# A two-layer network on one core: the first layer's normalisation in its own stretch of slot 6, other slots for its pieces, and the first fronts among the recurrence's last lead steps

## The chip, the core and the metric

The kernel runs on one core of a Trainium2 chip. The core has five engines, each with an instruction queue of its own that is worked off in order: TensorE (PE, matrix products; its weight loads are listed apart as PEld), VectorE (DVE), ScalarE (ACT, tabulated functions), GpSimd (POOL) and SyncE (SP), which here only issues DMA transfers. The engines meet at semaphores. The metric is the device time of one execution in microseconds; the time before is the median of three runs.

## The reference

The input is x, 4 images of 128 channels on 64 by 64 points. Two layers are computed, each with a spatial and a token part, all with residual connections:

```
x = x + conv0(ln_c(x))                 # deformable neighbourhood attention
t = t + recurrence(ln_t(t))            # y_t = sigmoid(wx_t + y_{t-1} V^T), 4096 tokens in turn
x = x + mamba(ln_c(x))                 # 8 state-space layers in turn
t = t + experts(ln_t(t))               # 64 experts, 8 tokens of the sequence each
```

Three parts matter here. The recurrence is a chain of 4096 steps for 4 images, each a 128 by 128 product and a sigmoid (in the kernel a tanh). The mamba part takes the recurrence's result, normalises it over the channels (mean, variance, division by the root of the variance plus 1e-6), and sends it through 8 layers. Each layer projects to 2 times 256 channels, convolves 4 taps along the tokens, applies silu, projects to dt, B and C, and runs for each of 256 channels and 16 states the scan h = exp(dt A) h + dt x B along all 4096 tokens; the output is the sum of h C over the states plus D x, gated with silu(z), projected back to 128 channels and put through an RMS norm. After the eighth layer the result is added to the mamba part's input. All is float32.

## The kernel before

**Stages.** `conv_layer` runs first (to about 1.65 ms), then `mamba`, which carries the recurrence with it, then `experts`. In `conv_layer` and `mamba` the order of each engine's instructions is the order in which they are written (`tc.manual_schedule`), so queues can be followed in the code. Waits between engines, and those for a buffer to come free, are put in by the framework. A buffer of a tag with one copy is given to a new tile once all uses of the tile before are done, uses written further down among them.

**Bodies.** Tokens are cut into 8 chunks of 512 (`TL`). A body is one chunk of one layer of one image; 8 x 8 x 4 = 256 bodies run in the order chunk, layer, image. The main loop runs over bodies i, and each iteration has 16 slots j. `o` is the body whose scans run (i), `n` the next, whose front is computed meanwhile, `q` the last, which is finished, and `s` and `z` are the bodies two and three on, if they are in the first layer: those must be fetched and normalised from the recurrence's result, while other layers take the RMS norm's result `us[b]`. `m` is the body two on in any layer, `a` is any body that exists.

In each slot the loop writes: `decay(o, j+2)` (two exponentials on ScalarE), `inputs(o, j+1)` (16 small matmuls into PSUM, the tile dBx; in slots 6 and 7 instead exponentials into the same buffers, dAp, since GpSimd makes the inputs of that pair of states), a recurrence step where `STEPS[j]` is over 0, `scan(o, j)` (two scans on VectorE), after odd j `times_c` (a copy of the last states, then a 128x2048 product on GpSimd that waits for the two scans), the left side of PLAN's row j, `add_up` (eight transposing matmuls that add states to yT), the right side of the row, and a second step where `STEPS[j]` is 2.

**PLAN** is the hand-written table of the remaining pieces, one row per slot, as `who.piece`. The pieces that matter here: `v0`, `v1` project the convolution's input, and ScalarE takes it from the bank with the last tap, then three one-column operations (L851) that add what the previous chunk's last tokens give (`edge`, eight small GpSimd operations, L829 to L836), then a copy of the tail (L855); the `tap` pieces on VectorE (L860) follow. `pz`, `silu`, `silu_z` make the gate; `pd`, `keep` project to dt, B, C; `pt`, `softplus` make dt (L928); `dtx` is the product dt x on GpSimd (L934), `turn` its transposition (L941, then ScalarE L944), `diag` makes diagonal matrices of B for dBx. `po` is the output projection (L1086), `square` reads it twice on ScalarE (L1092, L1094), `pm`, `log`, `rstd`, `u` are the RMS norm (L1098 to L1109), `end` adds the mamba input after the last layer (a load on SP, a GpSimd sum L1115, a store). `s.mean` is the mean's matmul, the subtraction (L812) and the square; `s.var` the variance's matmul (L818) and its logarithm (L819), `s.rstd` the exponential of it, `s.u` the product (GpSimd, L1109). `ln` and `exp` load ScalarE's tables (L1126) for logarithm with exponential, and for exponential with tanh.

**Banks.** Two PSUM banks, f0 and f1, serve all pieces; `BANK` says which takes which. `square` must have read f0 (po) before `pz0` may write it.

**Recurrence.** `rec.step(t)` is a matmul of two instructions (L669) and a tanh (L672), each waiting for the other. Every 64 steps one matmul (L664) puts the inputs into PSUM, and after the last of them GpSimd forms y and the sum (L678, L679) and SP stores it to `x2_d`. Body 0 needs the first 512 tokens; `PRE` = 576 steps run before any of the mamba part. Then bodies 0 and 1 are fetched and normalised, and the `n` pieces of PLAN are run through once for body 0, before the main loop.

Of the kernel before, what the change touches and what calls it, by code (L numbers as in the profile page):

```python
# [9 lines left out]
AF = mybir.ActivationFunctionType  # L10
# [10 lines left out]
B = 4  # L21
# [24 lines left out]
TL = 512  # L46
# [8 lines left out]
PRE = 512 + RT  # L55
# [555 lines left out]
class Recurrence:  # L611
# [78 lines left out]


PLAN = """
n.v0 |
s.mean |
| n.tap03 n.tap02 o.C3
n.v1 | q.leave1 o.by0
n.tap01 | o.by1 q.back1
q.gate1 |
| n.tap12 q.po0 n.tap13 n.tap11
q.po1 | q.square n.pz0 n.pz1 n.silu n.silu_z0 n.silu_z1 a.exp  # L700
n.pd0 | n.pd1 n.keep
n.pt0 n.C2 n.pt1 | n.softplus0 q.pm n.softplus1 a.ln q.log q.rstd s.var s.rstd a.exp
n.dtx0 n.bt n.B |
q.u s.u | o.leave0 n.diag0
q.end n.turn0 n.skip0 n.skip1 | n.diag2
o.back0 n.diag5 | n.diag3
n.diag1 z.fetch n.C0 o.gate0 n.dtx1 m.edge | n.C1
n.diag4 n.turn1 n.diag6 |
""".strip().split("\n")
STEPS = [1, 0, 1, 2, 1, 1, 1, 0, 1, 0, 1, 0, 2, 2, 2, 1]  # L710

BANK = {
    "v0": 0, "v1": 1, "pz0": 0, "pz1": 1, "pd": 0, "pt0": 1, "pt1": 0, "bt": 0, "turn0": 1,
    "turn1": 1, "back0": 1, "back1": 0, "po": 0, "pm": 1, "mean": 1, "var": 1,
}


# [9 lines left out]
def mamba(tc, ops, I, rec, x2_d, x3_d):  # L727
# [8 lines left out]
    nc = tc.nc  # L736
# [5 lines left out]
    with ExitStack() as ctx:  # L742
# [41 lines left out]
        def bank(what):  # L784

            name = f"f{BANK[what]}"
            return psf.tile([P, TL], F32, tag=name, name=name)

        def where(j):

            h, sp = divmod(j, SP)
            return (sp if h == 0 else SP - 1 - sp), h
# [5 lines left out]
        def load(l):  # L798
            given = wp.tile([P, W_GIVEN], F32, tag="given", name="given")
            nc.sync.dma_start(out=given, in_=I["m_given"][l])  # L800
            weights[l] = given


        def fetch(o):
            o.x2 = w1.tile([P, TL], F32, tag="x2", name="x2")
            nc.sync.dma_start(out=o.x2, in_=x2_d[:, o.b, o.ck * TL : (o.ck + 1) * TL])
# [8 lines left out]
        def var(o):  # L815
            o.r = w1.tile([P, TL], F32, tag="r0", name="r0")
            v = bank("var")
            nc.tensor.matmul(v, ops.avg, o.x2, start=True, stop=True)  # L818
            nc.scalar.activation(o.r, v, AF.Ln, bias=ops.eps6)  # L819


        def edge(o):

            o.edge = w.tile([P, NH, DC - 1], F32, tag="edge", name="edge")
            part = w.tile([P, NH, DC - 1, DC - 1], F32, tag="part", name="part")
            for h in range(NH):
                tl = tail[:, o.l, o.b, h, :]
                for k in range(DC - 1):
                    nc.gpsimd.tensor_tensor(  # L829
                        part[:, h, k, :],  # L830
                        tl[:, k : k + DC - 1],
                        taps[:, o.l, h, k : k + 1].to_broadcast([P, DC - 1]),
                        ALU.mult,
                    )
            nc.gpsimd.tensor_tensor(o.edge, part[:, :, 0, :], part[:, :, 1, :], ALU.add)
            nc.gpsimd.tensor_tensor(o.edge, o.edge, part[:, :, 2, :], ALU.add)  # L836
# [132 lines left out]
        def exps(o, j):  # L969
            sp, h = where(j)  # L970
            for k in range(2):
                n = 2 * sp + k
                nc.scalar.activation(  # L973
                    o.dA[j][:, k, :], o.dt[h], AF.Exp, scale=A[:, o.l, h, n : n + 1]
                )

        def decay(o, j):
            if where(j)[0] != SP_B:
                o.dA[j] = dap.tile([P, 2, TL], F32, tag="dA", name="dA")
                exps(o, j)  # L980
# [141 lines left out]
        def get(i):  # L1122
            return bodies[i] if 0 <= i < len(bodies) else None

        def table(name):
# [12 lines left out]
        pieces |= {f"by{h}": lambda o, h=h: times_b(o, SP - 1 + h) for h in range(NH)}  # L1138
        pieces |= {f"C{g}": lambda o, g=g: give_c(o, g) for g in range(NS // 4)}
        pieces |= {  # L1140
            "fetch": fetch, "mean": mean, "var": var, "silu": silu_x, "keep": keep, "B": give_b,
            "bt": turn_b, "square": square, "pm": rms, "log": log, "rstd": rstd, "u": norm,
            "end": lambda o: end(o) if o.l == DEPTH - 1 else None, "edge": edge,
            "exp": table(EXP_TANH), "ln": table(EXP_LN),
# [7 lines left out]
                    pieces[what](who[k])  # L1152

        load(0)
        for t in range(PRE):
            rec.step(t)
        for s in bodies[0:2]:
            for what in ("fetch", "mean", "var", "rstd", "u"):
                pieces[what](s)
        fetch(bodies[2])  # L1160
        edge(bodies[0])
        for row in plan:
            for part in row:
                for k, what in part:
                    if k == "n":
                        pieces[what](bodies[0])
        decay(bodies[0], 0)
        decay(bodies[0], 1)
        edge(bodies[1])
        inputs(bodies[0], 0)  # L1170
        LAG = 4
        t = PRE
        for i in range(len(bodies) + 1):
            o, n, q, s = get(i), get(i + 1), get(i - 1), get(i + 2)
            who = {"o": o, "n": n, "q": q, "m": s, "a": o or q}
            z = get(i + 3)
# [172 lines left out]
@with_exitstack  # L1349
def tile_kernel(ctx: ExitStack, tc: tile.TileContext, I, out):  # L1350
    nc = tc.nc
    const = ctx.enter_context(tc.tile_pool(name="const", bufs=1))
    dram = ctx.enter_context(tc.tile_pool(name="scratch", bufs=1, space=DRAM))
    nc.scalar.preload_act_table_set(EXP_LN)
    ops = Ops(nc, const)
    stats = const.tile([P, B * NBLK, 6], F32, name="stats")
    x1_d = dram.tile([P, B, L], F32, name="x1_d")
    x2_d = dram.tile([P, B, L], F32, name="x2_d")
    x3_d = dram.tile([P, B, L], F32, name="x3_d")
    wx_d = dram.tile([P, B, L], F32, name="wx_d")  # L1360

    with tc.manual_schedule(), ExitStack() as c:
        conv_layer(tc, ops, I, x1_d, wx_d, stats)
        rec = Recurrence(c, tc, ops, I, stats, wx_d, x1_d, x2_d)
        mamba(tc, ops, I, rec, x2_d, x3_d)
    experts(tc, ops, I, x3_d, out)
# [88 lines left out]
```

## Time and profile before

| | |
|---|---|
| median of 3 runs | 16217.22 us (16211.93 to 16219.21) |
| profiled execution | 16205.68 us, span 16203.7 us |
| PE busy | 14711.5 us (91%) |
| DVE busy | 13670.0 us (84%) |
| POOL busy | 13219.3 us (82%) |
| ACT busy | 12120.7 us (75%) |
| scans, L1028 (8192) | 9931 us, 1.26 us each |
| times_c, L1044 (2048) | 9298.0 us, 4.54 us each |
| table loads, L1126 (771) | 989.2 us, 1.283 us each |
| waits of L818 for the logarithm L1102 | 108.3 us over 58 waits (PE and PEld) |
| waits of L941 for dtx | 244.3 us (PE) |
| waits of scans for dBx | 1012.0 us |

A busy time is the sum over an engine's instructions; it is an average over stages, so a share of 84% in the whole can be no gap at all in one stage. The lists of instructions in order of time, one engine at a time, show for each group its start, its duration, its line, what it writes and reads, how many were merged, and in brackets how long the engine stood idle before it and which engine's instruction ended that. "issue" is idle time that no recorded event explains.

### The profile page before, as it was taken

The page shows a single profiled execution, that of the slowest core. Times are in us where ns is not written, and L with a number is a line of the kernel's source. Part 1 is how long each engine was busy: PE and PEld are TensorE (multiplying, and loading weights), DVE is VectorE, ACT ScalarE, POOL GpSimd, SP SyncE. Part 2 cuts the span into 40 slices and gives each one's busy share as a digit, 9 for nine tenths or more (in the row PEclk, how much of TensorE's full clock was granted, in tenths as well). Part 3 has the DMA queues.
Part 4 walks back from the last instruction along what each step waited for, and adds up shares of the span by engine and source line. Part 5 has one row for each costly group of instructions (what it writes and reads, how often), then busy time and mean ns, then how long its engine had stood idle before and what let it go on. Part 6 is the DMA issues. An engine that isn't in the chain of part 4 may idle for free. (4 is left out here: it accounts for less than half of the span.)

```text
span 16203.7 us, 303591 instructions
## 1 busy us (share of the span) xinstructions
PE 14711.5 (91%) x120710; PEld 11053.2 (68%) x120710; DVE 13670.0 (84%) x14929; ACT 12120.7 (75%) x23622; POOL 13219.3 (82%) x9102
## 2 busy tenths in 40 slices
PE   7889689999999999999999999999999999899967
PEld 3444567777777777777777777777777777666636
DVE  8988059998999899989998999889998999899931
ACT  6887258887888788878887888778877887777750
POOL 4554059998999899989999999999998999899940
PEclk8999579999999999999999999999999999999975
DMA  0000012222222222222222222222222222222214
GB/s 21 24 22 20 14 67 101 100 100 99 101 101 101 97 101 101 101 99 98 101 101 103 98 98 100 107 97 99 100 101 102 99 101 97 103 97 99 95 47 121
DMA packets 461738, 1431.35 MB, mean 88 GB/s; under 512 B 205472, under 2 KB 238880, under 8 KB 329120
## 3 DMA queue, kind: packets, MB, share of 16 engines
q1 hardware_dynamic: 460320, 1411.92, 24.4%
q8 instruction: 953, 15.61, 0.4%
q14 instruction: 465, 3.81, 0.1%
HBM read 1353.04 MB, written 58.72 MB: 87 GB/s over the span
## 5 line engine op out<-in xcount | busy, mean ns | idle before, releaser
L1028 DVE TENSOR_TENSOR_SCAN hs<-dA,state,dBx 128x512 f32<-128x512 f32 x7168 | 8702.5, 1263 | 1048.8 <-PE dBx L995 1012.0
L1044 POOL TENSOR_TENSOR hs<-hs,Cb 128x2048 f32<-128x2048 f32 x2048 | 9298.0, 4540 | 166.2 <-POOL state L1041 1.3
L973 ACT ACTIVATE dA<-dt,A 128x512 f32<-128x512 f32 x7168 | 4737.3, 722 | 7.3 <-DVE hs L1028 1.1
L1048 PE MATMUL yT<-ident,hs 128*128 128x128 f32 x32768 | 4349.1, 277 | 7.5 <-POOL hs L1044 7.5
L1048 PEld LDWEIGHTS yT<-ident,hs 128*128 128x128 f32 x32768 | 3794.6, 144 | 770.5 <-issue 643.4
L995 PE MATMUL dBx<-diag,dtxT 64*128 64x128 f32 x57344 | 4188.7, 285 | 122.2 <-DVE hs L1028 109.8
L995 PEld LDWEIGHTS dBx<-diag,dtxT 64*128 64x128 f32 x57344 | 3514.8, 188 | 1085.7 <-issue 711.3
L672 ACT ACTIVATE z<-p 128x4 f32<-128x4 f32 x4096 | 711.6, 174 | 1844.5 <-PE p L669 1838.8
L669 PE MATMUL p<-z,vt 128*128 128x4 f32 x8192 | 1578.9, 263 | 205.6 <-ACT z L672 203.7
L669 PEld LDWEIGHTS p<-z,vt 128*128 128x128 f32 x8192 | 1350.6, 207 | 588.0 <-ACT z L672 304.3
L1016 POOL TENSOR_TENSOR hs<-Bb,dtx 128x512 f32<-128x512 f32 x1024 | 1275.3, 1279 | 0.2 <-PE yT L1048 0.2
L1028 DVE TENSOR_TENSOR_SCAN hs<-dAp,state,hs 128x512 f32<-128x512 f32 x1024 | 1228.5, 1262 | 0.0
L961 DVE TENSOR_TENSOR diag<-f,i 128x512 f32<-128x512 f32 x1792 | 1158.5, 671 | 8.0 <-PE f L949 8.0
L860 DVE SCALAR_TENSOR_TENSOR xc<-f,taps,xc 128x509 f32<-128x509 f32 (+2 forms) x1536 | 1131.0, 736 | 37.6 <-ACT tail L855 10.4
L1041 POOL COPY state<-hs 128x4 f32<-128x4 f32 x2048 | 389.5, 190 | 832.0 <-DVE hs L1028 831.1
L1126 ACT ACT_TABLE_LOAD x771 | 989.2, 1283 | 10.4
L278 DVE SCALAR_TENSOR_TENSOR acc<-qp,dww,acc 128x512 f32<-128x512 f32 x1184 | 888.0, 750 | 12.2
L973 ACT ACTIVATE dAp<-dt,A 128x512 f32<-128x512 f32 x1024 | 708.8, 692 | 212.2 <-DVE hs L1028 180.1
L875 PE MATMUL f<-u,given 128*128 128x512 f32 x1024 | 510.8, 621 | 330.2 <-ACT pos L1094 323.2
L849 ACT ACTIVATE xc<-f,taps 128x509 f32<-128x509 f32 x512 | 350.4, 684 | 474.4 <-PE f L846 472.2
L934 POOL TENSOR_TENSOR dtx<-dt,xc 128x512 f32<-128x512 f32 x512 | 651.8, 1273 | 12.1 <-ACT dt L928 12.1
L944 ACT COPY dtxT<-f 128x512 f32<-128x512 f32 x512 | 298.3, 583 | 448.4 <-PE f L941 448.4
(222 smaller groups left out, 16824.6 us busy)
## 6 DMA issues: line engine op xcount, KB each, us to landing
Cb<-c_d SPq DMA_DIRECT2D x1024, 1024.0 KB, 4.7
Bb<-c_d SPq DMA_DIRECT2D x256, 512.0 KB, 5.5
given<-in_m_given_dram SPq DMA_DIRECT2D x64, 640.0 KB, 5.9
x<-x_d SPq DMA_DIRECT2D x128, 256.0 KB, 2.8
w<-in_w_dram SPq DMA_DIRECT2D x128, 256.0 KB, 2.8
x_d<-x SPq DMA_DIRECT2D x64, 256.0 KB, 2.0
c_d<-dbl SPq DMA_DIRECT2D x512, 32.0 KB, 1.6
xb<-in_x_dram SPq DMA_DIRECT2D x32, 256.0 KB, 3.1
```

Of the source, the lines that this page charges most:

```text
L278: nc.vector.scalar_tensor_tensor(rows(to), x, dww[:, t : t + 1], rows(o.acc), ALU.mult, ALU.add)
L669: nc.tensor.matmul(self.p[:, k, :], self.vt, self.before, start=False, stop=True, skip_group_check=True)
L672: nc.scalar.activation(self.z[:, k, :], self.p[:, k, :], AF.Tanh, scale=0.5)
L860: nc.vector.scalar_tensor_tensor(x, o.v[h][:, : TL - k], taps[:, o.l, h, DC - 1 - k : DC - k], x, ALU.mult, ALU.add)
L961: nc.vector.tensor_tensor(o.diag[:, sp], bt.unsqueeze(2).to_broadcast([P, NB, 64, 2]), i64.unsqueeze(1).unsqueeze(3).to_broadcast([P, NB, ...
L973: nc.scalar.activation(o.dA[j][:, k, :], o.dt[h], AF.Exp, scale=A[:, o.l, h, n : n + 1])
L995: nc.tensor.matmul(o.dBx[j][:, at : at + 64, :], o.dtxT[h][row, n, :], o.diag[row, sp, n], start=True, stop=True,)
L1016: nc.gpsimd.tensor_tensor(hs[:, k, :].rearrange("p (q n t) -> p q n t", n=NB, q=2), o.Bb[:, k, :].rearrange("p (q n t) -> p q n t", n=NB, ...
L1028: nc.vector.tensor_tensor_scan(hs[:, k, :], o.dA[j][:, k, :], hs[:, k, :] if sp == SP_B else o.dBx[j][:, :, k], state[:, o.l, o.b, h, s : ...
L1044: nc.gpsimd.tensor_tensor(hs, hs, o.Cb[f], ALU.mult)
L1048: nc.tensor.matmul(o.yT[:, n, :], x[:, n * P : (n + 1) * P], ops.ident, start=start and n == 0, stop=True, is_transpose=True, skip_group_c ...
L1126: return lambda o: nc.scalar.preload_act_table_set(name)
```

## The change

In PLAN several pieces change their slots. `edge` is computed for the next body in slot 0 rather than for the body two on in slot 14. The variance's matmul moves from slot 9 to slot 6 and from bank f1 to f0; its logarithm is a piece of its own, `lnv`, and stands with its exponential between two table loads (`s.ln`, `s.exp`) in slot 6. `s.u` moves from slot 11 to slot 14, behind `dtx1`; `end` from slot 12 to slot 14, ahead of `dtx1`; the fetch of the first layer's next body from slot 14 to slot 8. Before the main loop only 512 steps of the recurrence run alone. The other 64 are written two at a time after the normalisation of bodies 0 and 1 and after each part of PLAN's rows for body 0; the table loads of the rows (`a` pieces) are run there too, and one after each of the two normalisations.

```diff
 PLAN = """
-n.v0 |
+n.edge n.v0 |
 s.mean |
 | n.tap03 n.tap02 o.C3
 n.v1 | q.leave1 o.by0
 n.tap01 | o.by1 q.back1
 q.gate1 |
-| n.tap12 q.po0 n.tap13 n.tap11
+s.var | n.tap12 q.po0 n.tap13 s.ln s.lnv s.rstd s.exp n.tap11
 q.po1 | q.square n.pz0 n.pz1 n.silu n.silu_z0 n.silu_z1 a.exp
-n.pd0 | n.pd1 n.keep
-n.pt0 n.C2 n.pt1 | n.softplus0 q.pm n.softplus1 a.ln q.log q.rstd s.var s.rstd a.exp
+n.pd0 | z.fetch n.pd1 n.keep
+n.pt0 n.C2 n.pt1 | n.softplus0 q.pm n.softplus1 a.ln q.log q.rstd a.exp
 n.dtx0 n.bt n.B |
-q.u s.u | o.leave0 n.diag0
-q.end n.turn0 n.skip0 n.skip1 | n.diag2
+q.u | o.leave0 n.diag0
+n.turn0 n.skip0 n.skip1 | n.diag2
 o.back0 n.diag5 | n.diag3
-n.diag1 z.fetch n.C0 o.gate0 n.dtx1 m.edge | n.C1
+n.diag1 q.end n.C0 o.gate0 n.dtx1 s.u | n.C1
 n.diag4 n.turn1 n.diag6 |
...
-    "turn1": 1, "back0": 1, "back1": 0, "po": 0, "pm": 1, "mean": 1, "var": 1,
+    "turn1": 1, "back0": 1, "back1": 0, "po": 0, "pm": 1, "mean": 1, "var": 0,
...
             nc.tensor.matmul(v, ops.avg, o.x2, start=True, stop=True)
-            nc.scalar.activation(o.r, v, AF.Ln, bias=ops.eps6)
+            o.var = v
+
+        def log_var(o):
+            nc.scalar.activation(o.r, o.var, AF.Ln, bias=ops.eps6)
...
         load(0)
-        for t in range(PRE):
-            rec.step(t)
+        t = 0
+        def steps(n):
+            nonlocal t
+            for t in range(t, min(t + n, PRE)):
+                rec.step(t)
+                t += 1
+        steps(TL)
         for s in bodies[0:2]:
-            for what in ("fetch", "mean", "var", "rstd", "u"):
+            for what in ("fetch", "mean", "var", "lnv", "rstd", "u", "exp"):
                 pieces[what](s)
+            steps(2)
         fetch(bodies[2])
         edge(bodies[0])
         for row in plan:
             for part in row:
                 for k, what in part:
-                    if k == "n":
+                    if k in ("n", "a"):
                         pieces[what](bodies[0])
+                steps(2)
+        steps(PRE)
```

More of the change, by code (lines that the diff above doesn't have):

```diff
@@ L1140, in mamba @@
         pieces |= {
-            "fetch": fetch, "mean": mean, "var": var, "silu": silu_x, "keep": keep, "B": give_b,
+            "fetch": fetch, "mean": mean, "var": var, "lnv": log_var, "silu": silu_x, "keep": keep, "B": give_b,
             "bt": turn_b, "square": square, "pm": rms, "log": log, "rstd": rstd, "u": norm,
@@ L1171, in mamba @@
         LAG = 4
-        t = PRE
         for i in range(len(bodies) + 1):
```

## The prediction

> **What bounds the kernel now.** I read the page, then the waits, then the timeline engine by engine. The chain that ended last covers only the closing experts stage and says nothing of the edits. The 256 bodies fill 2203 to 15640 us. I measured their lengths by the ACT copy of L895, one per body: an ordinary body takes 50.8 us (every fourth 51.5; mean 50.97), and the five around each turn from the last layer to the first take 54.7, 58.3, 59.0, 60.2 and 55.6 (means of the turns). A turn so costs 33 us more than five ordinary bodies, and there are seven. Slots are PLAN's rows, from 0.
>
> VectorE, first an ordinary body, then twice one with first-layer pieces (start us, us, engine, line, tiles; in brackets the idle time before it and who ended it):
>
> ```profile
> 8057.47 2.45 DVE L1028 TENSOR_TENSOR_SCAN hs<-dA,state,dBx 128x512 f32<-128x512 f32 x2 [2.58 <-PE dBx L995]
> 8777.00 2.45 DVE L1028 TENSOR_TENSOR_SCAN hs<-dA,state,dBx 128x512 f32<-128x512 f32 x2 [5.16 <-PE dBx L995]
> 8798.12 2.45 DVE L1028 TENSOR_TENSOR_SCAN hs<-dA,state,dBx 128x512 f32<-128x512 f32 x2 [2.18 <-PE dBx L995]
> ```
>
> Between these waits, one of 0.74 and, in first-layer bodies, that of L812, VectorE runs without a gap, so it bounds the body, and what delays a dBx lengthens it. What delays them, on TensorE:
>
> ```profile
> 8774.66 1.12 PE L818 MATMUL f<-x,avg 128*128 128x512 f32 x2 [1.45 <-ACT r L1102]
> 8794.05 1.12 PE L941 MATMUL f<-ident,dtx 128*128 128x128 f32 x4 [3.29 <-POOL dtx L934]
> 8072.09 0.66 PE L941 MATMUL f<-ident,dtx 128*128 128x128 f32 x4 [0.50 <-POOL dtx L934]
> ```
>
> In slot 9 the variance matmul waits 1.45 us for the logarithm that frees its bank and runs 1.1: the 2.58 us by which 5.16 exceeds the ordinary wait. In slot 15 turn1 waits for dtx1, which GpSimd reaches late because s.u and q.end (1.28 us each) stand before it: 3.29 against 0.50 us.
>
> The 2.58 that every body has comes from slots 7 to 9. TensorE is full there and starts when ScalarE has emptied po's bank:
>
> ```profile
> 8757.82 0.15 ACT L672 ACTIVATE z<-p 128x4 f32<-128x4 f32 x1
> 8757.88 1.32 ACT L973 ACTIVATE dA<-dt,A 128x512 f32<-128x512 f32 x2
> 8759.41 1.42 ACT L973 ACTIVATE dAp<-dt,A 128x512 f32<-128x512 f32 x2 [0.21 <-DVE hs L1028]
> 8760.76 0.58 ACT L1092 ACTIVATE sq<-f 128x512 f32<-128x512 f32 x1
> 8761.24 0.68 ACT L1094 ACTIVATE pos<-f,rmsw 128x512 f32<-128x512 f32 x1
> ```
> ```profile
> 8758.01 1.88 PE L1086 MATMUL f<-y,given 128*128 128x512 f32 x4
> 8761.97 1.98 PE L875 MATMUL f<-u,given 128*128 128x512 f32 x4 [1.21 <-ACT pos L1094]
> ```
>
> ScalarE has 0.21 us of slack between slot 6's tanh and the square. From pz0 (8761.97) to dBx of slot 10, TensorE has no gap.
>
> **The skill.** "ScalarE: Activation LUTs", What ACT_TABLE_LOAD costs: a load takes about 1283 ns and a drain of 1380 comes on top. The trace has 1283 ns for each load and the next activation right behind it (load at 8770.05, softplus at 8771.34), so I use 1.28. "TensorE: Matmul & The Clock Gate", What's actually happening: idle windows of about 3.4 us halve the clock until a busy one has passed. The trace agrees in size: after the 3.29 us gap the granted clock was 0.50 from 8793.7 to 8796.9, and turn1, the additions and a dBx took 1.4 us longer. Step-by-step: what each phase is for, in the same page: matmuls stay in program order, only weight loads are pulled ahead. So a held po0 holds po1 and all behind it.
>
> **The change part by part.**
>
> *Variance to slot 6, 30 bodies.* Gone from slot 9: matmul and wait, −2.58 us on VectorE. New in slot 6, on ScalarE between tanh and decay: Ln table 1.28 + Ln 0.70 (start to next start) + Exp 0.65 + Exp table 1.29 = 3.92, less the slack 0.21, so square, pos, pz0 and every dBx behind them come 3.71 us later. TensorE is no cover: var now shares bank 0 with po, and q.po0 is issued before s.lnv reads it, so po0 must wait for that Ln: tanh ends at 8757.9, table to 8759.2, Ln to 8759.9, po0 at 8759.93 instead of 8758.01. That wait is inside the 3.71. Net 30 × (3.71 − 2.58) = +34 us.
>
> *TensorE's clock in the new gap.* From 8762.6 (additions end) to 8765.7 (pos ends) TensorE idles 3.06 us instead of 1.21, after 0.97 us before po0. The trace has both outcomes: all 18 gaps of 3.3 us before turn1 slowed it, gaps of 2.1 to 2.7 about two in three, the 29 gaps of 1.7 before pz0 none. A slow stretch costs 1.4 us. Bounds 0 and 30 × 1.5 = 45; I take eight in ten: 30 × 0.8 × 1.4 = +34.
>
> *s.u to slot 14 behind dtx1, q.end to slot 14 ahead of it.* s.u no longer delays dtx1; q.end still does, by 1.28 us. The body that has q.end alone takes 54.7 us: 3.75 over the mean, in which s.mean (0.69, and 1.76 waiting for its matmul) and 1.10 from dtx1 are. Take 2.58 from the others' excess: 4.8, 5.5, 6.7, 2.0 us. They should fall to about 3.75, 4.1, 4.7 and 0. That is 6.3 us a turn × 7 = 44, and 1.3 in each of the two first-layer bodies at the start: −47. u is needed by v0 four TensorE instructions after turn1, some 4 us; s.u adds 1.28: hidden. q.end's store on SP now stands before C0 and C1 and waits until 8792.6; C0 lands in 4.7 us (median), its product starts at about 8801: hidden, by some 3 us. z.fetch (slot 8) only moves a load into a buffer that the variance has freed: nothing.
>
> *Edge from slot 14 of the body before last to slot 0 of the last, some 255 times.* GpSimd, ScalarE and VectorE before:
>
> ```profile
> 8073.18 0.20 POOL L836 TENSOR_TENSOR edge<-edge,part 128x6 f32<-128x6 f32 x1
> 8073.32 0.19 POOL L1041 COPY state<-hs 128x4 f32<-128x4 f32 x1
> 8073.59 4.54 POOL L1044 TENSOR_TENSOR hs<-hs,Cb 128x2048 f32<-128x2048 f32 x1
> 8078.88 0.19 POOL L1041 COPY state<-hs 128x4 f32<-128x4 f32 x1 [0.75 <-DVE hs L1028]
> ```
> ```profile
> 8076.69 0.83 ACT L851 ACTIVATE xc<-f,edge,taps 128x1 f32<-128x1 f32 x3
> 8081.07 1.50 DVE L860 SCALAR_TENSOR_TENSOR xc<-f,taps,xc 128x509 f32<-128x509 f32 x2
> ```
>
> The product now starts 0.35 us earlier, and the eight small operations (1.35 us) run behind it, until 8079.1, mostly in the 0.75 us gap. ScalarE's L851 must wait for them: 2.4 us of new idle per body, with two decays and a tanh queued behind. The taps on VectorE need L855, then done at 8080.1, and start at 8081.07: cover 0.95 us (0.8 in every fourth body). The decay for slot 3 ends at 8081.2, needed at 8082.5; the next TensorE step comes 0.4 us later and meets a 0.34 us wait. So nothing, as long as that cover holds; each 0.1 us beyond it costs 25 us. A gain is excluded: VectorE has no gap there to close.
>
> *The front.* Now 64 steps of 0.853 us run alone, then 44.4 us of fronts until the first scan:
>
> ```profile
> 2158.68 0.17 ACT L672 ACTIVATE z<-p 128x4 f32<-128x4 f32 x1 [0.68 <-PE p L669]
> 2203.05 4.79 DVE L1028 TENSOR_TENSOR_SCAN hs<-dA,state,dBx 128x512 f32<-128x512 f32 x4 [0.67 <-ACT dA L973]
> ```
>
> From step 511 (2103.3) that is 99.7 us. At most 54.6 could go. But a step is a round trip TensorE–ScalarE, both in order, and the fronts are mostly such round trips too: two steps after each part stand between one part and the next. Walking it through with the row durations: the load waits for its store and the first mean starts at +6.3; both normalisations with the Exp loads and four steps end at +28.5; v0 to +32; ten steps to +40; v1 after two more, to +45; eighteen steps to +60; pz and silu to +67; and so on with two steps a part to the last at +105.6, turn1, dBx and the first exponential at +107.5. Hidden are the taps, diags, dtx and u; added are five table loads (6.4 us) less one. I get +8 at the half clock that these rows have; at full clock each step costs 0.2 less (13 in all) and the larger matmuls together some 8 less, so −13. I take +4, between the two and near the first, since the lead's rows show the half clock throughout.
>
> Sum: 34 + 34 − 47 + 4 = +25 us on the profiled execution's 16205.7 (span 16203.7), 16231. The median lies 11.5 above that execution: 16242, +0.15%.
>
> **The rivals.**
> 1. *The clock stays up in the new gap and in the front* (for: the 29 gaps of 1.7; against: 3.06 is nearer 3.3). 34 − 47 − 13 = −26: 16191.
> 2. *The steps hide in the front.* For: VectorE and GpSimd idle there. Against: the steps wait on the same two queues. If some 40 of the 54.6 us go: 34 + 34 − 47 − 40 = −19 (16198), and about −50 (16165) with the clock up.
> 3. *Slower: the edge wait breaks its cover.* If L855 comes 0.3 us later than the taps need it in all 255 bodies: 25 + 76 = +101, 16318. It decides from 0.95 us, which is half of the 1.9 to 2.4 us that ScalarE is held. For: two queues run in series before it. Against: both margins come from a very regular trace.
> That the pieces don't move as written is no rival: nothing reorders a queue.
>
> **How the numbers follow.** Forecast 0.55, own range 16217 to 16267; rival 1 0.18, rival 2 0.13, rival 3 0.14. Within 0.2% (32 us, about what a measurement of this kernel can tell from no change): 0.40 + 0.15 + 0.03 = 0.58. Faster: 0 + 0.03 + 0.10 = 0.13. Slower: 0.15 + 0.14 = 0.29. The range leaves out the ends of rivals 2 and 3, half of each and a little: 16187 to 16285.
>
> **What would show it.** Slot 9: L818 no longer waits for L1102 (108 us in all over both parts). Slot 6: L1086 waits about 1 us for r of L819, L875 about 3 us for pos in those bodies. VectorE's 5.16 us become 7 to 8.4; its 2.18 become 1.1. L1126 loads go from 771 to 836. ACT L851 waits for edge some 500 us in all, with L860 not waiting. First scan at 2199 to 2211. Wrong it would be if po0 doesn't wait, if L860 waits for L855, or if the first scan comes before 2190.

## The result and the profile after

The changed kernel takes 16239.8 us (median of 22 runs, 16225.9 to 16253.3), the kernel before 16211.3 us (22 runs on the same chip, 16200.5 to 16220.6): a ratio of 1.0018, 95% interval 1.0011 to 1.0024, or 28.5 us more. The forecast was 16242, 25 us over the 16217.2 from which it set out.

The profiled execution of the changed kernel took 16244.5 us with a span of 16242.7, 39.0 more than the span before. Not all of that belongs to the change: the stages outside the recurrence and the bodies vary by some 20 us between executions (2430 to 2454 us in the thirteen traces). So I use a second measure, **the loop**: from the start of the first lead step's tanh (L672) to the start of the ACT copy of the last body (L898, before it was L895). It went from 13767.2 (1660.7 to 15427.9) to 13798.5 us (1657.5 to 15456.1), +31.3. Line numbers from about L820 on are 3 higher than before.

**First-layer bodies.** VectorE (timeline: start us, us, engine, line, tiles; in brackets the idle time before it and who ended it), from slot 8 to slot 0, in the turn that the prediction showed:

```profile
8790.69 2.46 DVE L1031 TENSOR_TENSOR_SCAN hs<-dAp,state,hs 128x512 f32<-128x512 f32 x2 [0.73 <-ACT dAp L976]
8794.86 2.45 DVE L1031 TENSOR_TENSOR_SCAN hs<-dA,state,dBx 128x512 f32<-128x512 f32 x2 [1.71 <-PE dBx L998]
8799.03 2.45 DVE L1031 TENSOR_TENSOR_SCAN hs<-dA,state,dBx 128x512 f32<-128x512 f32 x2 [1.72 <-PE dBx L998]
8804.08 2.45 DVE L1031 TENSOR_TENSOR_SCAN hs<-dA,state,dBx 128x512 f32<-128x512 f32 x2 [2.59 <-PE dBx L998]
...
8824.20 2.45 DVE L1031 TENSOR_TENSOR_SCAN hs<-dA,state,dBx 128x512 f32<-128x512 f32 x2 [1.14 <-PE dBx L998]
```

The 5.16 us wait is 2.59, as in the other bodies, but the three scans ahead of it wait 0.73, 1.71 and 1.72 us (before: nothing, nothing and 0.74), and the wait for turn1's dBx is 1.14 instead of 2.18. ScalarE and TensorE in that slot 6 and 7, and pz0 (L878) in the next bodies of the turn:

```profile
8784.01 1.28 ACT L1129 ACT_TABLE_LOAD   x1
8785.31 0.69 ACT L822 ACTIVATE r<-f,eps 128x512 f32<-128x512 f32 x1
...
8786.66 1.28 ACT L1129 ACT_TABLE_LOAD   x1
...
8791.00 0.68 ACT L1097 ACTIVATE pos<-f,rmsw 128x512 f32<-128x512 f32 x1
```
```profile
8786.05 1.98 PE L1089 MATMUL f<-y,given 128*128 128x512 f32 x4 [0.95 <-ACT r L822]
...
8791.74 1.98 PE L878 MATMUL f<-u,given 128*128 128x512 f32 x4 [2.83 <-ACT pos L1097]
...
8819.91 0.66 PE L944 MATMUL f<-ident,dtx 128*128 128x128 f32 x4 [1.72 <-POOL dtx L937]
...
8909.35 3.67 PE L878 MATMUL f<-u,given 128*128 128x512 f32 x4 [2.83 <-ACT pos L1097]
```

The load, Ln, Exp and load stand between tanh and decay, po0 waits 0.95 us for Ln (so the shared bank holds it), pz0 waits 2.83 us for pos. Behind the same 2.83 us gap the four matmuls of pz take 1.98 us in one body and 3.67 in another (2.42 and 1.98 in the turn's other two): TensorE's clock fell in some bodies and not in others (the last section shows what tells them apart). Turn1's wait is 1.72 us where it was 3.29.

**Ordinary bodies.** GpSimd, ScalarE, VectorE and TensorE of the body that answers to the one shown before (timeline lines of the four engines):

```profile
8103.43 0.20 POOL L839 TENSOR_TENSOR edge<-edge,part 128x6 f32<-128x6 f32 x1
...
8103.66 0.84 ACT L854 ACTIVATE xc<-f,edge,taps 128x1 f32<-128x1 f32 x3 [2.33 <-POOL edge L839]
...
8105.57 1.51 DVE L863 SCALAR_TENSOR_TENSOR xc<-f,taps,xc 128x509 f32<-128x509 f32 x2
8106.99 4.93 DVE L1031 TENSOR_TENSOR_SCAN hs<-dA,state,dBx 128x512 f32<-128x512 f32 x4
...
8107.11 0.39 PE L669 MATMUL p<-z,vt 128*128 128x4 f32 x2 [0.16 <-ACT z L672]
...
8109.17 0.28 PE L669 MATMUL p<-z,vt 128*128 128x4 f32 x2
```

ScalarE stands for 2.33 us until GpSimd has the edge. The taps (L863) start 1.91 us after L854 began and show no wait. But TensorE's first lead step of slot 3 waits for the tanh behind the decays (the 0.16). Behind it come v1, the additions (8108.30 to 8109.34) and the second step of slot 3 (from 8109.17). Scans 3 and 4, which took 4.78 us together before, take 4.93: between them VectorE waits 0.15 us. In the list of waits (what waited for what: us in total, times, longest):

```profile
ACT xc L854 <- POOL edge L839: 481.3, 246, 3.1
...
DVE hs L1031 <- PE p L669: 27.6, 58, 2.9
```

The second line was 23.2 us in 56 waits before; it holds the bodies that are every fourth, since the list leaves out waits as short as 0.15 us. It names the step p because that is the last TensorE record to end before the scan starts; a scan reads nothing of p.

**The front.** The first scan:

```profile
2203.16 4.79 DVE L1031 TENSOR_TENSOR_SCAN hs<-dA,state,dBx 128x512 f32<-128x512 f32 x4 [16.99 <-ACT dA L976]
```

It comes 545.6 us after the first lead step, against 542.3 before (2203.05 − 1660.7).

Body by body, the 144 ordinary bodies between turns are on average 0.135 us longer (medians 50.79 and 50.94), the 56 that are every fourth 0.00, and the seven turns together +8 us (from the third body before each to the third after).

### The profile page after: what moved, and what is told of

Its sections match the earlier page's. It is cut to its first block, busy times and chain, and to the rows that moved or that the text cites. A ratio compares the mean times of both kernels' runs of the same rounds, so it can differ in the third digit from the quotient of the medians.

```text
span 16242.7 us, 303653 instructions
## 1 busy us (share of the span) xinstructions
PE 14734.5 (91%) x120710; PEld 11051.3 (68%) x120710; DVE 13690.2 (84%) x14929; ACT 12179.8 (75%) x23686; POOL 13213.2 (81%) x9118
## 5 line engine op out<-in xcount | busy, mean ns | idle before, releaser
L998 PE MATMUL dBx<-diag,dtxT 64*128 64x128 f32 x57344 | 4201.4, 286 | 82.9 <-DVE hs L1031 55.8
L998 PEld LDWEIGHTS dBx<-diag,dtxT 64*128 64x128 f32 x57344 | 3526.0, 189 | 1053.3 <-issue 728.4
L672 ACT ACTIVATE z<-p 128x4 f32<-128x4 f32 x4096 | 709.8, 173 | 1568.0 <-PE p L669 1561.8
L1031 DVE TENSOR_TENSOR_SCAN hs<-dAp,state,hs 128x512 f32<-128x512 f32 x1024 | 1231.7, 1263 | 22.5 <-ACT dAp L976 20.3
L863 DVE SCALAR_TENSOR_TENSOR xc<-f,taps,xc 128x509 f32<-128x509 f32 (+2 forms) x1536 | 1130.6, 736 | 49.9 <-ACT tail L858 22.7
L878 PE MATMUL f<-u,given 128*128 128x512 f32 x1024 | 532.8, 645 | 368.1 <-ACT pos L1097 368.1
L854 ACT ACTIVATE xc<-f,edge,taps 128x1 f32<-128x1 f32 x1536 | 426.9, 350 | 481.4 <-POOL edge L839 481.3
```

The costliest lines, as they stand in the source:

```text
L672: nc.scalar.activation(self.z[:, k, :], self.p[:, k, :], AF.Tanh, scale=0.5)
L863: nc.vector.scalar_tensor_tensor(x, o.v[h][:, : TL - k], taps[:, o.l, h, DC - 1 - k : DC - k], x, ALU.mult, ALU.add)
L998: nc.tensor.matmul(o.dBx[j][:, at : at + 64, :], o.dtxT[h][row, n, :], o.diag[row, sp, n], start=True, stop=True,)
L1031: nc.vector.tensor_tensor_scan(hs[:, k, :], o.dA[j][:, k, :], hs[:, k, :] if sp == SP_B else o.dBx[j][:, :, k], state[:, o.l, o.b, h, s : ...
```

## The experiments

Each kernel was timed beside the kernel before, 4 to 22 executions each. "Timed" is the difference of medians with the interval of the ratio; "loop" is the difference of the loop in one profiled execution to the 13767.2 us of before; a difference in the loop so rests on two single executions.

| kernel | timed, us | ratio, 95% | loop, us |
|---|---|---|---|
| changed kernel | +28.5 | 1.0011 to 1.0024 | +31.3 |
| e_edge: edge alone | +29.7 | 1.0011 to 1.0025 | +24.0 |
| e_var: variance alone | +66.1 | 1.0029 to 1.0054 | +56.3 |
| e_u: u and end to slot 14 | −39.7 | 0.9967 to 0.9985 | −60.5 |
| e_front: front alone | +10.9 | 0.9997 to 1.0014 | +1.2 |
| a_noedge: changed, edge put back | +10.1 | 1.0000 to 1.0017 | +7.9 |
| a_by0: changed, by0 in slot 4 | −17.2 | 0.9982 to 0.9999 | −19.6 |
| a_pz: changed, pz1 first | +20.2 | 1.0005 to 1.0018 | +22.0 |
| b_u2_by0 | −157.8 | 0.9891 to 0.9918 | −155.4 |
| best2 | −191.0 | 0.9870 to 0.9897 | −190.0 |
| best_pz | −193.4 | 0.9866 to 0.9896 | −190.2 |
| best_pz_tap | −56.8 | 0.9951 to 0.9976 | −54.7 |

### One part at a time

**The edge alone** (e_edge):

```diff
-n.v0 |
+n.edge n.v0 |
...
-n.diag1 z.fetch n.C0 o.gate0 n.dtx1 m.edge | n.C1
+n.diag1 z.fetch n.C0 o.gate0 n.dtx1 | n.C1
```

> The kernel before with the edge's move alone. Theory A, the prediction's step: the wait of ScalarE for the edge stays within its cover, 0 us (within 5). Theory B, read from the two traces (ordinary bodies of the changed kernel are 0.13 us longer, because scan 4 waits 0.15 us for the additions behind the second lead step of slot 3): 160 ordinary bodies by 0.13 us, +21 us (15 to 27), and the bodies that are every fourth unchanged. The rival of a broken cover at the taps said +76 us; for that VectorE's L860 would have to wait for L855.

Measured +24.0 in the loop and +29.7 timed. The ordinary bodies are 0.161 us longer (144 of them, +23.2), every fourth 0.01, and the turns unchanged (+0.7 together). Theory B holds; "nothing" is refuted, and so is the rival that broke the taps' cover: three times too large, and L860 does not wait.

**The variance alone** (e_var):

```diff
-| n.tap12 q.po0 n.tap13 n.tap11
+s.var | n.tap12 q.po0 n.tap13 s.ln s.lnv s.rstd s.exp n.tap11
...
-... a.ln q.log q.rstd s.var s.rstd a.exp
+... a.ln q.log q.rstd a.exp
...
-"mean": 1, "var": 1,
+"mean": 1, "var": 0,
```

> The kernel before with the variance in slot 6 alone (its product, logarithm and both table loads; bank 0 instead of 1; its load stays in slot 14). Theory A, the prediction's step: +34 us from the later square and +34 from TensorE's clock in the new gap, +68 in all (55 to 79). Theory B: the clock is up again before a dBx is late, so that only +34 us remain (25 to 45). Theory C, from the seven turns of the changed kernel, which together grew by 7 us where the moved normalisation was to give back 44: about +45 to +55 us.

Measured +66.1 timed, +56.3 in the loop, +55.1 of it in the seven turns. B's 34 is too small: the clock's share is real. The loop lies at the border of A and C and the timed value within A, so these two are not told apart. pz0 and the scan of slot 9 in this kernel:

```profile
8786.62 3.31 PE L878 MATMUL f<-u,given 128*128 128x512 f32 x4 [2.84 <-ACT pos L1097]
8791.38 2.45 DVE L1031 TENSOR_TENSOR_SCAN hs<-dA,state,dBx 128x512 f32<-128x512 f32 x2 [3.35 <-PE dBx L998]
```

After a gap of 2.84 us pz takes 3.31 us instead of 1.98, the granted clock is 0.50 from 8787.4 to 8790.4, and VectorE waits 3.35 instead of 1.71 us. A wait of 3 us or more is there in 25 of the 28 first-layer bodies of the turns, 25 × 1.64 = 41 us, near the 34 allowed. In all, the waits of scans 8 to 11 grow by 63 us in the turns, and those behind turn1 (its dBx and the mean) shrink by 16. In the changed kernel only 18 of 28 wait 3 us or more.

**u and end to slot 14** (e_u):

```diff
-q.u s.u | o.leave0 n.diag0
-q.end n.turn0 n.skip0 n.skip1 | n.diag2
+q.u | o.leave0 n.diag0
+n.turn0 n.skip0 n.skip1 | n.diag2
...
-n.diag1 z.fetch n.C0 o.gate0 n.dtx1 m.edge | n.C1
+n.diag1 z.fetch q.end n.C0 o.gate0 n.dtx1 s.u m.edge | n.C1
```

> The kernel before with GpSimd's normalisation of the first layer (u) in slot 14 behind dtx1 and the last layer's addition (end) ahead of dtx1 in slot 14, nothing else. Theory A, the prediction's step: -47 us (-40 to -52), with VectorE's wait of 2.18 us for turn1's copy at about 0.7 to 1.1 us. Theory B: in slot 14 the addition delays dtx1 by as much as before and turn1 by more, since there is less room up to slot 15: -20 us or less.

Measured −39.7 timed (by the interval −24 to −53), −60.5 in the loop, −53.5 of it in the turns. The five bodies of a turn fall from 54.6, 58.3, 58.9, 60.1, 55.5 to 54.5, 57.1, 57.6, 57.3 and 53.4 us. B's "−20 or less" is refuted; A's −47 lies between the two measures.

**The front alone** (e_front), with the plan of before (var is split into var and lnv, which stay side by side in slot 9):

```diff
-for t in range(PRE):
-    rec.step(t)
+steps(TL)
 for s in bodies[0:2]:
-    for what in ("fetch", "mean", "var", "rstd", "u"):
+    for what in ("fetch", "mean", "var", "lnv", "rstd", "u", "exp"):
         pieces[what](s)
+    steps(2)
...
-            if k == "n":
+            if k in ("n", "a"):
                 pieces[what](bodies[0])
+        steps(2)
+steps(PRE)
```

> The kernel before with the front's pieces between the lead steps alone. Theory A, the prediction's step: +4 us (-13 to +8), first scan at 2199 to 2211 us. Theory B, from the changed kernel's trace, where the first scan came at 2203.2 against 2203.1 us: 0 us (within 5), nothing of the 44 us of fronts hidden. The rival of hidden steps said -40 us.

The first scan comes 547.0 us after the first lead step, 4.7 later than before. (As a clock time it is 2215.0, outside the expected 2199 to 2211, since the lead itself began 7.3 us later in this execution.) The eight kernels that keep the front of before have this distance at 542.3 to 546.8, the five with the new front at 545.6 to 547.1: A's +4 and B's 0 are not told apart. What is shown is that nothing near the 40 us of the rival is hidden. The loop is at +1.2, and timed the difference can't be told from none.

### Where the edge's cost goes

**by0 in slot 4** (a_by0). The four hs buffers are handed out in the order in which the code first asks for a group. by0 asks for group 3 in slot 3, before scan 4 asks for group 2. Group 2 then gets the buffer of the body before's group 7, whose last additions run in slot 3: behind the first lead step of that slot and v1, and ahead of the second step (the expectations, here and of e_edge, have them behind it).

```diff
-n.v1 | q.leave1 o.by0
-n.tap01 | o.by1 q.back1
+n.v1 | q.leave1
+n.tap01 | o.by0 o.by1 q.back1
```

> The changed kernel with the product by0 issued in slot 4 ahead of by1 instead of in slot 3. GpSimd's order stays the same; only the order in which the four hs buffers are handed out changes: scan 4 then takes the buffer of the body before's group 6, whose last additions are in slot 1, instead of group 7's, whose last additions are in slot 3 behind the second lead step. Theory B (the edge's cost reaches VectorE through that buffer): against the changed kernel the 0.14 us in each ordinary body go (-23 us), and the 0.36 us that scan 4 waits in every fourth body before the change too (56 of them, -20 us): -23 to -43, that is -15 to +6 against the kernel before. Theory C (the edge costs through dBx of slot 5 or the taps): no difference, +28 against the kernel before.

Measured −17.2 against before, −50.9 in the loop against the changed kernel: B's two parts as expected, and 8.4 us more in the turns, for which nothing was expected. The ordinary bodies are back at 50.79 (−0.003 against before) and every fourth falls by 0.40 us on average, −22.5 in all. Every fourth body had this scan 4 in the kernel before (first line) and in the changed one:

```profile
8645.71 2.45 DVE L1028 TENSOR_TENSOR_SCAN hs<-dA,state,dBx 128x512 f32<-128x512 f32 x2 [0.36 <-PE p L669]
8671.52 2.45 DVE L1031 TENSOR_TENSOR_SCAN hs<-dA,state,dBx 128x512 f32<-128x512 f32 x2 [0.36 <-PE p L669]
```

and with by0 moved, an ordinary body and the same every-fourth one:

```profile
8081.50 4.79 DVE L1031 TENSOR_TENSOR_SCAN hs<-dA,state,dBx 128x512 f32<-128x512 f32 x4
...
8640.95 4.79 DVE L1031 TENSOR_TENSOR_SCAN hs<-dA,state,dBx 128x512 f32<-128x512 f32 x4
```

Scans 3 and 4 follow each other in 4.79 us in both. ScalarE waits for the edge as long as ever (488.6 us in 246 waits), and VectorE's waits for p are down from 58 (27.6 us) to 2 (5.9 us).

GpSimd's and TensorE's orders are the same in both kernels, so the edge's delay reaches VectorE through that one buffer: edge, L854, two decays, tanh, the first lead step of slot 3, v1, additions, scan 4. Theory C is refuted.

**The edge put back** (a_noedge: the changed kernel with m.edge behind s.u in slot 14, no n.edge):

```diff
-n.edge n.v0 |
+n.v0 |
...
-n.diag1 q.end n.C0 o.gate0 n.dtx1 s.u | n.C1
+n.diag1 q.end n.C0 o.gate0 n.dtx1 s.u m.edge | n.C1
```

> The changed kernel with the edge back in slot 14 of the body before last. If the parts add up: -23 us against the changed kernel, about +5 us against the kernel before (-5 to +15). If the edge's cost shows only with the other parts beside it or hides some of theirs: anything outside that.

+7.9 in the loop and +10.1 timed, 23.4 under the changed kernel's loop: the edge adds to the other parts and hides nothing of them, to within the spread of single executions.

### What the last layer's addition costs

**u and end both behind dtx1, by0 in slot 4** (b_u2_by0, from the kernel before):

```diff
-q.u s.u | o.leave0 n.diag0
-q.end n.turn0 n.skip0 n.skip1 | n.diag2
+q.u | o.leave0 n.diag0
+n.turn0 n.skip0 n.skip1 | n.diag2
...
-n.diag1 z.fetch n.C0 o.gate0 n.dtx1 m.edge | n.C1
+n.diag1 z.fetch n.C0 o.gate0 n.dtx1 s.u q.end m.edge | n.C1
```

with by0 as above.

> The kernel before with u and the last layer's addition both behind dtx1 in slot 14, and by0 in slot 4. From the run with u alone moved: -45 (between its timed -40 and its trace's -53 in the turns); the addition behind dtx1 takes TensorE's wait for dtx from 2.06 to about 0.5 us in three to four bodies of each of seven turns, 7 x 3.5 x 1.5 = -37 (if all of it reaches VectorE; 0 if none does); by0 takes the 0.36 us of scan 4 in every fourth body, -20. Together -100 (-45 to -110).

Measured −157.8, more than the most that was expected: −124.8 in the turns and −24.7 in every fourth body. So end, moved behind dtx1, is worth another 124.8 − 53.5 = 71 us, twice the 37 expected. Turn1, v0 behind it and the subtraction of the next first-layer mean (L812), first with end ahead of dtx1 (TensorE, VectorE):

```profile
8760.06 0.66 PE L941 MATMUL f<-ident,dtx 128*128 128x128 f32 x4 [2.06 <-POOL dtx L934]
8764.10 2.05 PE L846 MATMUL f<-u,given 128*128 128x512 f32 x2
8770.26 0.69 DVE L812 TENSOR_TENSOR xm<-x,f 128x512 f32<-128x512 f32 x1 [3.96 <-issue]
```

then with end behind dtx1 too:

```profile
8712.95 0.66 PE L941 MATMUL f<-ident,dtx 128*128 128x128 f32 x4 [0.85 <-POOL dtx L934]
8715.75 1.10 PE L846 MATMUL f<-u,given 128*128 128x512 f32 x2
8719.97 0.69 DVE L812 TENSOR_TENSOR xm<-x,f 128x512 f32<-128x512 f32 x1 [0.34 <-issue]
```

TensorE's wait for dtx falls from 2.06 to 0.85, and VectorE's wait for the mean from 3.96 to 0.34 us. Two things add up here. TensorE comes 1.2 us earlier out of turn1. And its clock stays up: in the first kernel it was at 0.50 from 8761.3 to 8768.2, behind the gap, and v0 took 2.05 us instead of 1.10. With end ahead of dtx1 the clock falls so in 21 of the 28 bodies, and VectorE then waits 3.45 us on average for turn1's dBx and the mean, against 1.79 in the 7 others; with end behind it the clock falls in 2 of 28, and the wait is 0.48 in the others. The hold so gives about 28 × (1.79 − 0.48) = 37 us, as expected, and the clock some 21 × (3.45 − 1.79) = 35, which the expectation had not counted.

**The variance's product in slot 2** (best2, on top of that):

```diff
-| n.tap03 n.tap02 o.C3
+| n.tap03 n.tap02 s.var o.C3
...
-... a.ln q.log q.rstd s.var s.rstd a.exp
+... a.ln q.log q.rstd s.lnv s.rstd a.exp
...
-nc.scalar.activation(o.r, v, AF.Ln, bias=ops.eps6)
+nc.scalar.copy(o.r, v)
+
+def log_var(o):
+    nc.scalar.activation(o.r, o.r, AF.Ln, bias=ops.eps6)
```

> The same with the variance's product in slot 2, behind the mean's, and a copy of it to SBUF on ScalarE there, so that slot 9 holds only its logarithm and exponential and no product that waits for the bank. The 2.58 us more that VectorE waits for dBx in slot 10 of a first-layer body should go: 30 x 2.58 = -77 against the kernel just named; the copy (about 0.65 us) and the product (1.1 us) in slot 2 cost between 0 and 30 x 0.65 = 20 us. So -57 to -77 against it, -100 to -185 against the kernel before, likeliest -165. If the product's wait in slot 9 was not what lengthens those bodies: no gain over it.

Measured −191.0 against before (16019.0 us), and 34.6 us less loop than b_u2_by0, where 57 to 77 were expected. The 5.16 us wait is 2.58, as expected, but a wait that was not there takes 1.22 back (ScalarE and VectorE):

```profile
8739.03 0.71 ACT L822 ACTIVATE r<-r,eps 128x512 f32<-128x512 f32 x1
...
8742.52 2.45 DVE L1031 TENSOR_TENSOR_SCAN hs<-dA,state,dBx 128x512 f32<-128x512 f32 x2 [1.22 <-ACT dA L976]
```

The variance's Ln and Exp now delay the exponential that the scan of slot 12 needs.

### What sets the pace of slots 6 to 8

**pz1 ahead of pz0**, in the changed kernel (a_pz), in best2 (best_pz), and with an earlier tap (best_pz_tap):

```diff
-q.po1 | q.square n.pz0 n.pz1 n.silu ...
+q.po1 | q.square n.pz1 n.pz0 n.silu ...
```
```diff
-q.gate1 |
-| n.tap12 q.po0 n.tap13 n.tap11
+q.gate1 | n.tap12
+| q.po0 n.tap13 n.tap11
```

(the second for best_pz_tap alone).

> The changed kernel with pz1 issued ahead of pz0. pz1 needs neither po's bank nor pos, only bank 1, free when the last tap has ended, so it runs in the gap in which TensorE waits for pos. In first-layer bodies of the changed kernel that gap (2.84 us, the clock at 0.50 behind it in 17 of 28) becomes about 1.9 in two pieces. If the clock's dip is what makes VectorE's wait 3.35 instead of 1.71 us there: all 28 waits at 1.71 or below, -17 x 1.65 = -28 us; if the 3.35 has another cause they stay. In ordinary bodies the last tap ends at 8095.43 and pos at 8095.76, so pz1 and pz0 end 0.44 us earlier and with them every product up to slot 10: up to 255 x 0.44 = -112. Together -60 to -140 against the changed kernel, -30 to -110 against the kernel before.

> The faster kernel of the last call (u and the addition behind dtx1, by0 in slot 4, the variance's product in slot 2) with pz1 ahead of pz0. Up to 0.44 us in each body, if the 2.58 us wait for dBx in slot 10 follows from when pz0 and pz1 end: -112 against it, about -300 against the kernel before (-190 if another dependency takes over at once).

> The same with the tap tap12 in slot 5 instead of slot 6, so that the last tap ends 0.7 us earlier and pz1 starts right behind the additions, with 1.2 us of gap to fill. Then pz0 starts with pos and both end 0.94 us earlier than without the swap; pd0 needs silu's result, which allows 0.78. Up to 255 x 0.78 = -200 against the kernel without the swap, about -390 against the kernel before; no gain over the last one if the scan of slot 6, which comes 0.7 us later, delays the additions or a dBx by as much.

None of the hoped-for gains came; best_pz is at the −190 that its expectation named for another dependency taking over at once. The ordinary bodies don't move: a_pz 50.94 as the changed kernel, best_pz at 50.78 with the same waits of 0.74 and 2.58 us. In best_pz pz ends 0.34 us earlier, but the dBx behind it (L998) now waits:

```profile
8013.45 1.16 PE L998 MATMUL dBx<-diag,dtxT 64*128 64x128 f32 x16 [0.38 <-DVE hs L1031]
```

It starts at the same distance from the body's ACT copy (4.21 us) as before, because the scan that frees its buffer has not moved. pd0 doesn't move either (2.88 us before that copy in both). ScalarE has no gap from the exponentials of slot 7 (in the kernel before, 8093.25) to that copy (8102.06); that it sets the pace here is likely, and these runs don't show it by themselves. With the tap moved, the loop loses 135 us against best_pz: the ordinary bodies are at 51.34, with waits of 1.31 and 2.70 us where there were 0.74 and 2.58, and pd0 waits 0.40 us for gate.

In the first-layer bodies of a_pz the gap is split, but the clock falls all the same, in 22 of 28 bodies (18 in the changed kernel):

```profile
8788.54 1.13 PE L878 MATMUL f<-u,given 128*128 128x512 f32 x2 [1.97 <-ACT pos L1097]
8789.60 1.80 PE L998 MATMUL dBx<-diag,dtxT 64*128 64x128 f32 x16
```

The dBx of slot 8 takes 1.80 us instead of 1.16 after gaps of 0.95 and 1.97 us. Scan 9 no longer waits 3.35 us (2.48 at most), but in 7 bodies scan 10 now waits 3.75 to 4.08 instead of 1.72. The waits of scans 8 to 11 are 1.5 us less in the turns, where 28 were expected, and the loop is 9.3 us less.

## Why the prediction was right, and where it wasn't

The total was right: 16242 against 16239.8, within 0.2% as the likeliest case said, and +25 against +28.5 as a difference. Its steps were not all, and that the sum came so close is luck: to its +25 the parts one by one add 24 for the edge and take off 12 for the variance, 13.5 for u and 3 for the front.

- **Edge: "So nothing, as long as that cover holds".** This step failed: 24 us. The waits on GpSimd, the 2.4 us on ScalarE and the unbroken cover at L860 came as written. The sentence "the next TensorE step comes 0.4 us later and meets a 0.34 us wait" was true of dBx of slot 5 (the step came 0.22 us later), but between that step and that dBx stand v1, the additions and the second step, and the additions free the hs buffer that scan 4 writes. The trace of before showed that this had no slack: in every fourth body scan 4 already waited 0.36 us at that place. I had followed the delay to the next wait on TensorE and not to everyone who waits for TensorE in between.
- **Variance: +34 and the clock +34.** Met: 56 to 66 us where 68 was summed. The bank, the 0.95 us of po0 and the gap before pz0 are in the trace (2.83 for 3.06). The clock falls after 18 (changed) to 25 (alone) of 28 gaps and costs 1.64 us each; I had taken eight in ten and 1.4. In scans 8 to 11 alone the 68 are 63; what is below that comes from shorter waits behind turn1, which the sum did not have.
- **s.u behind dtx1: −47.** Between the −40 timed and the −61 of the loop. One cost is not named in this term and one premise was wrong. The cost is TensorE's clock behind the gap before turn1: it fell in 27 of 28 bodies before and in 21 of e_u, where VectorE waits 1.7 us more in each of them. The 3.75 us of a body with end alone were split into 1.10 from dtx1 and 1.76 of the mean's matmul, as if the second were the mean's own price. In b_u2_by0 those bodies wait about 0.25 us for the mean: most of the 1.76 was end's, and the change, which keeps end ahead of dtx1, leaves it there.
- **Front: +4.** The first scan is 3.3 us later in the changed kernel, 4.7 in the front alone; kernels with the old front spread over 4.5 us, so the +4 is neither shown nor refuted. That nothing is hidden fits the argument that the lead step is a round trip on the same two queues; no run tests it further.
- **The sum.** In loops, edge, variance, u and front alone give 24.0 + 56.3 − 60.5 + 1.2 = +21.0, the whole +31.3. The edge is not where the rest lies (23.4 by taking it out); the other three leave 7.9 together and −3.0 as a sum. Of these 11 us only 2 are in the turns (55.1 − 53.5 + 0.0 as a sum, 3.6 together). About 5 are in the last two bodies, which in every kernel but e_edge are 2.3 to 3.2 us shorter than in the one trace of before, so that three differences count it three times. About 5 are in the first four bodies, and for these interaction and spread stay open.

Rival 1 (the clock stays up) is refuted for two in three of the bodies, rival 2 (steps hide) by the first scan, rival 3 by L863, which doesn't wait in the bodies.

## What to carry to other kernels

When a wait is put on an in-order queue, follow the delay to every instruction behind it and to every buffer that those free, not only to the next wait that has room: a wait of a few tenths that already shows in some bodies marks the place without slack. Which buffer a tile gets depends on the order in which tiles are first asked for, so moving a request by one slot, with the engines' order unchanged, took away some 0.14 us in each ordinary body and 0.40 in every fourth. Work that nobody needs soon belongs behind the operation that others wait for; here moving the last layer's addition behind dtx1 gained 71 us, about half of it because the shorter gap (0.85 us for 2.06) left TensorE's clock up.

## What the runs showed of the hardware

After the same gap of 2.83 us, in the same code, TensorE's clock fell or stayed: pz took 1.98, 2.42, 3.67 and 1.98 us in one turn of the changed kernel. The clock's own record in the traces tells these cases apart. Every stretch at 0.50 begins on a grid of 3.413 us that runs through the whole execution (the same step in all thirteen traces, every start within 0.01 us of it) and lasts one or more of its steps. The clock falls for a step when TensorE did little in the step before, by the records of its matmuls. For the four bodies:

| pz starts | the step of the grid in which most of the gap lies | TensorE busy in it, us of 3.41 | clock in the next step | pz, us |
|---|---|---|---|---|
| 8791.74 | 8789.91 to 8793.32 | 1.58 | 1.00 | 1.98 |
| 8849.94 | 8847.94 to 8851.35 | 1.41 | 0.50 | 2.42 |
| 8909.35 | 8905.96 to 8909.38 | 0.59 | 0.50 | 3.67 |
| 8969.23 | 8967.40 to 8970.82 | 1.59 | 1.00 | 1.98 |

From 2300 to 15400 us of the changed kernel the clock falls at 58 steps; before 56 of them TensorE was busy for at most half of a step (0.50, rounded). Of the 3718 steps in which it stays up, 8 follow such a step, the first and the last of the table among them. With the variance alone it is 67 of 70, and 7 of 3695. The border is not sharp in these records: between 0.43 and 0.57 of a step both occur. So it is not the length of one gap that counts but how much idle time falls into one step, and a step need not be idle throughout, as the prediction took it: half idle is enough. A gap of 2.83 us can be split by the grid and leave the clock up, and a gap of 1.97 us that lies in one step can bring it down: in a_pz TensorE was busy for 1.44 us of the step from 8786.53 to 8789.94, and the dBx behind it took 1.80 us instead of 1.16. Where the gaps fell on the grid differed from kernel to kernel: behind the gap before pz the clock fell in 25 of 28 bodies with the variance alone, 25 with the edge put back, 21 with by0 moved and 18 in the changed kernel, each counted in one execution.
